# The gated MLP's 42 leftover features as two row tiles, their activations held twice on the partitions

## The chip, the cores and the metric

The kernel runs on one core of a Trainium2 chip. The metric is the device time of one execution in microseconds, as the median of several runs. A core has a matrix engine (TensorE, PE), three engines for elementwise work (VectorE or DVE, ScalarE or ACT, GpSimd or POOL) and a queue for transfers (SyncE or SP). TensorE reads its operands from SBUF, a memory of 128 partitions, and writes to PSUM, which has eight banks of 512 f32 numbers on every partition.

## The reference

The program is an adaptive-norm block on x of shape (2, 2048, 256) in f32: a three-layer transformer with linear attention, then a two-layer transformer with local attention and a gated MLP. The change touches the gated MLP of the second part. Cut to it:

```python
HID = int(256 * 4 * 2 / 3)                  # 682
for l in range(2):
    x = x + local_attention(...) @ wo
    h = layernorm(shift_token(x))
    h = h @ w1 + b1                         # 256 -> 2 * 682
    a, g = jnp.split(h, 2, axis=-1)
    h = a * gelu(g)
    x = x + h @ w2 + b2                     # 682 -> 256
```

682 hidden features are five chunks of 128 and one of 42: `HID_CH = [128] * 5 + [42]`. The 42 are the leftover features of the title.

## The kernel before

The first part (linear attention) takes the first half of the time and is not touched. The second part keeps activations with features on the partitions: a stream tile `s` holds 512 tokens of one batch element, in two halves of 128 features each (`KT = 2`). There are 2 batch elements with 4 blocks of 512 tokens (`B`, `NB`, `TB`), so 8 blocks in each of the two layers.

The MLP (`mlp`, from L1107) walks over tiles (b, n, f): block by block, and in a block over the six chunks f. For each chunk TensorE computes the gate `pg` and the value `pa` from the stream (L1130, two contraction steps each). For the last chunk gate and value stand in one product `pg` of 106 rows: the value on partitions 0 to 41, the gate on 64 to 105 (`G_AT = 64`). ScalarE applies Gelu to the gate (L1138) into a tile `ge`, and VectorE multiplies it with the value plus its bias (L1139), also into `ge`.

The second product (`second`, L1164) multiplies chunk f of `w2` with `ge` and adds it up over the six chunks in two PSUM tiles `acc`, one for each half m of the 256 output features. It is issued one tile late: TensorE's order is the first products of tile i, then the second products of tile i - 1. So between the making of the last `ge` of a block and its use stands the first product of the next block's first chunk. After f = 5, `finish_block` adds `acc`, the bias and the residual on VectorE (L1081, once for each half). In layer 0 the sum is the next layer's stream. In layer 1 it is scaled on ScalarE (L1088), and one tile later `write_block` turns it with eight transposes (`ztp`, L1098), adds the residual (L1102) and writes the result out.

`w2` is a tile of 128 partitions, six chunks and 256 columns. `load_w2` fills it with one transfer for the five full chunks (L198) and one for the 42 leftover rows on partitions 0 to 41 (L201), both on the SP queue: for layer 0 at the start of the second part, for layer 1 from `load_mlp_late` during that layer's attention.

The order on TensorE, VectorE, ScalarE and GpSimd in the second part is the order in which the program issues the instructions (`tc.manual_schedule`). Steps of attention and of the MLP are sorted by due times: `WHEN` for attention, `into`, `FEED` and `out_of` for the MLP. The MLP of layer 0 overlaps the end of its attention and the beginning of layer 1's attention, whose steps used in the prediction are the products `pqkv` (L785), their rotated and normed form `qk` (L854), its transposes `tp` (L864), the scores `sim` (L881) and the running maxima (L897). `sim` takes heads of 64 features in pairs, one on partitions 0 to 63 and one on 64 to 127.

Of the kernel before, what the change touches and what calls it, by code (L numbers as in the profile page):

```python
# [14 lines left out]
P = 128  # L15
KT = 2
# [23 lines left out]
def block_kernel(ctx: ExitStack, tc: tile.TileContext, t: dict, out: bass.AP):  # L40
    nc = tc.nc
# [108 lines left out]
    NFH = len(HID_CH)  # L150

    def load_attn(l):

        wqkv = shared.tile([P, ROOM], F32, tag="wa0", name="wqkv").rearrange("p (k n) -> p k n", k=KT)
        nc.sync.dma_start(wqkv, t["wqkv"][l].rearrange("(k p) n -> p k n", p=P))
        room = shared.tile([P, ROOM], F32, tag="wb0", name="rsn_wo")
        rsn = room[:, : nt * P].rearrange("p (t i d) -> p t i d", i=2, d=64)
        nc.sync.dma_start(rsn, t["rope_s"])
        room2 = shared.tile([P, ROOM], F32, tag="wa1", name="rc_qks")
        rc = room2[:, : nt * P].rearrange("p (t i d) -> p t i d", i=2, d=64)  # L160
        nc.sync.dma_start(rc, t["rope_c"])
        qks = room2[:, nt * P : nt * P + P].rearrange("p (i d) -> p i d", i=2)
        nc.gpsimd.dma_start(qks[:, 0, :], t["q_scale"][l].partition_broadcast(P))
        nc.gpsimd.dma_start(qks[:, 1, :], t["k_scale"][l].partition_broadcast(P))
        wo = room[:, nt * P : nt * P + (INNER // P) * D].rearrange("p (k n) -> p k n", n=D)
        nc.sync.dma_start(wo, t["wo"][l].rearrange("(k p) n -> p k n", p=P))
        return wqkv, rc, rsn, qks, wo

    def scale_tables(rc, rsn, qks):
        for hf in range(2):  # L170
            nc.gpsimd.tensor_tensor(
                rsn[:, :, :, 32 * hf : 32 * hf + 32],
                rsn[:, :, :, 32 * hf : 32 * hf + 32],
                qks[:, :, 32 * (1 - hf) : 32 * (1 - hf) + 32].unsqueeze(1).to_broadcast([P, nt, 2, 32]),
                ALU.mult,
            )
        nc.vector.tensor_tensor(rc, rc, qks.unsqueeze(1).to_broadcast([P, nt, 2, 64]), ALU.mult)


    AW, GW = HID_CH[0] * (NFH - 1), HID_CH[-1]  # L180
    G_AT = 64
# [14 lines left out]
    def load_w2(pool, l):  # L196
        w2 = pool.tile([P, NFH, D], F32, tag="w2", name="w2")
        nc.sync.dma_start(  # L198
            w2[:, : NFH - 1, :], t["w2"][l, :AW, :].rearrange("(k p) n -> p k n", p=P)
        )  # L200
        nc.sync.dma_start(w2[:GW, NFH - 1, :], t["w2"][l, AW:, :])  # L201
        return w2

    attn_w, mlp_w = {}, {}
# [2 lines left out]
    with ExitStack() as c1:  # L207
# [16 lines left out]
        with tc.tile_pool(name="pro", bufs=1) as pro:  # L224
# [8 lines left out]
            for l in range(LA):  # L233
# [3 lines left out]
                for room, at, name, kts, width in (  # L237
# [7 lines left out]
                    w = room[:, at : at + kts * width].rearrange("p (k n) -> p k n", k=kts)  # L245
# [446 lines left out]
    with ExitStack() as c2:  # L692
# [7 lines left out]
        def bank(name):  # L700
            return psum.tile([P, TB], F32, tag="ps", name=name, bufs=8)
# [21 lines left out]
        for i in range(2):  # L723
            nc.gpsimd.tensor_copy(win_r[:, i * P : (i + 1) * P], win[:, (1 - i) * P : (2 - i) * P])
        w2s = {0: load_w2(wp, 0)}
        streams = [entry, {}]
        mids = [{}, {}]
# [4 lines left out]
        def v(l, name, i=0, rows_=P):  # L732
            o = V_F + l * VF_N + VF[name] + i
            return vec[:rows_, o : o + 1]

        def load_mlp_late(l):
            mlp_w[l] = load_mlp(l)
            w2s[l] = load_w2(wp, l)
# [330 lines left out]
        def finish_block(l, b, n, acc):  # L1069
            y = mids[l][b, n]  # L1070
            last = l == LF - 1
            if not last:
                nxt = streams[l + 1]
                z = new_stream(b, n, nxt.get((b, n - 1)))
                zr = rows(z)
                nxt[b, n] = z
            else:
                z = work.tile([P, KT, TB], F32, tag="w4", name="z")
                zr = [z[:, 0, :], z[:, 1, :]]
            for m in range(KT):  # L1080
                nc.vector.scalar_tensor_tensor(  # L1081
                    zr[m], acc[m], v(l, "b2", m), rows(y)[m], ALU.add, ALU.add
                )
            if last:
                xt = work.tile([P, NCH, D], F32, tag="w4", name="xl")
                nc.sync.dma_start(xt, xmid[b, n])
                for m in range(KT):
                    nc.scalar.activation(zr[m], zr[m], AF.Identity, scale=mod[:, 5, m, b : b + 1])  # L1088
                return zr, xt

        def write_block(b, n, zr, xt):
            res = work.tile([P, NCH, D], F32, tag="w4", name="res")
            for c2_ in range(NCH // 2):
                tp = bank("ztp").rearrange("p (u d) -> p u d", u=2)
                for u in range(2):
                    c = 2 * c2_ + u
                    for m in range(KT):
                        nc.tensor.transpose(  # L1098
                            tp[:, u, m * P : (m + 1) * P], zr[m][:, c * P : (c + 1) * P], ident
                        )  # L1100
                half = slice(2 * c2_, 2 * c2_ + 2)
                nc.vector.tensor_tensor(res[:, half, :], tp, xt[:, half, :], ALU.add)  # L1102
            nc.sync.dma_start(
                out[b, n * TB : (n + 1) * TB, :].rearrange("(c p) d -> p c d", p=P), res
            )

        def mlp(l):  # L1107


            tiles = [(b, n, f) for b in range(B) for n in range(NB) for f in range(NFH)]  # L1110
            ge, ready = {}, None
            w1, w2 = mlp_w[l], w2s[l]
            for i, (b, n, f) in enumerate(tiles):
                if l + 1 < LF and i == NFH:
                    attn_w[l + 1] = load_attn(l + 1)
                if l + 1 < LF and i == 3 * NFH:
                    scale_tables(*attn_w[l + 1][1:4])
                hb, w = streams[l][b, n], HID_CH[f]
                pg = bank("pg")
                if f < NFH - 1:  # L1120
                    pa = bank("pa")
                    parts = ((pg, AW + f * P, P), (pa, f * P, P))
                    gate = pg
                else:
                    pa = pg
                    parts = ((pg, 2 * AW, G_AT + GW),)
                    gate = pg[G_AT : G_AT + w, :]
                for pt, off, m in parts:
                    for kt in range(KT):
                        nc.tensor.matmul(  # L1130
                            pt[:m, :],
                            w1[:, kt, off : off + m],
                            hb[:, kt * TB : (kt + 1) * TB],
                            start=(kt == 0),
                            stop=(kt == KT - 1),
                        )
                ge[i] = ap_.tile([P, TB], F32, tag="ge", name="ge", bufs=3)
                nc.scalar.activation(ge[i][:w, :], gate, AF.Gelu, bias=v(l, "b1g", f, w))  # L1138
                nc.vector.scalar_tensor_tensor(  # L1139
                    ge[i][:w, :], pa[:w, :], v(l, "b1a", f, w), ge[i][:w, :], ALU.add, ALU.mult  # L1140
                )
                if ready:
                    write_block(*ready)
                    ready = None
                if i > 0:
                    ready = second(l, i - 1, tiles[i - 1], ge.pop(i - 1), w2)
                yield
            if l + 1 < LF:
                nc.scalar.preload_act_table_set("natural_log_exp_and_others")
            ready = second(l, len(tiles) - 1, tiles[-1], ge.pop(len(tiles) - 1), w2)  # L1150
            if ready:
                yield
                write_block(*ready)
# [3 lines left out]
        def second(l, i, tile_, g, w2):  # L1157
            b, n, f = tile_
            w = HID_CH[f]
            if f == 0:  # L1160
                accs[0] = [bank("acc") for _ in range(KT)]
            acc = accs[0]
            for m in range(KT):
                nc.tensor.matmul(  # L1164
                    acc[m],
                    w2[:w, f, m * P : (m + 1) * P],
                    g[:w, :],
                    start=(f == 0),
                    stop=(f == NFH - 1),
                )  # L1170
            if f == NFH - 1:
                done = finish_block(l, b, n, acc)
                return done and (b, n, *done)
# [144 lines left out]
```

## Time and profile before

| What | Value |
|---|---|
| Median of three runs | 3013.61 us (3012.41 to 3014.05) |
| Time of the profiled execution | 3012.11 us |
| Its span from the first to the last instruction | 3010.3 us |
| TensorE busy | 2927.8 us, 97% |
| VectorE, ScalarE, GpSimd busy | 1679.1, 1345.9, 1065.0 us |
| Second products of the 128-feature chunks (L1164) | 320 records, 150.4 us busy |
| Second products of the 42-feature chunk (L1164) | 64 records, 31.7 us busy |
| Gate and value of the 42-feature chunk (L1130) | 64 records, 30.2 us busy |

A line of a group names source line, engine, operation, output and input tiles, the shape, the number of records, the busy time, and the mean length of one. An f32 product shows as two records. TensorE's records overlap, [...] so the busy time of a group says more than the mean length of a record. PEld is the loading of the stationary operand. In the chain of waits each line is a stretch of the path that ended last.

### The profile page before, as it was taken

Reading aid. Unit: us, or ns where it says so; the run is one execution under the profiler, and the core shown is the slowest. Engines: PE = TensorE matmul, PEld = TensorE weight load, DVE = VectorE, ACT = ScalarE, POOL = GpSimd, SP = SyncE. Lnnn points to the kernel's source line nnn. Section 1 sums busy time; section 2 is a strip of 40 time slices with the busy share of each in tenths; the row PEclk is TensorE's granted clock in tenths of the full one; section 3 lists DMA queues with packets and bytes.
Section 4 is the critical chain, followed back from the end, with each engine's and each line's share of the span. In section 5 each row is a group of like instructions: output and inputs, shape, how many; then the busy total and the mean of one; then the engine's idle time right before and its main releaser. Section 6 shows DMA issues by size and latency. Waiting matters only on the chain.

```text
span 3010.3 us, 49194 instructions
## 1 busy us (share of the span) xinstructions
PE 2927.8 (97%) x19356; PEld 2138.0 (71%) x19356; DVE 1679.1 (56%) x4178; ACT 1345.9 (45%) x3269; POOL 1065.0 (35%) x937
## 2 busy tenths in 40 slices
PE   6999999999999999999996999999999999999999
PEld 5788888888888888788883777775444777776444
DVE  5555565555565555655544777774224777774222
ACT  3333343334443343433333667665114667665211
POOL 2222233222332223322224666663002666663000
PEclk9999999999999999999997999999999999999999
DMA  5000010000100001001012000001000000000011
GB/s 183 1 1 1 1 39 19 1 1 1 36 22 1 1 1 36 22 1 43 16 41 76 1 2 1 1 2 57 0 0 10 20 1 2 1 1 8 28 42 35
DMA packets 37288, 57.10 MB, mean 19 GB/s; under 512 B 3693, under 2 KB 28609, under 8 KB 36545
## 3 DMA queue, kind: packets, MB, share of 16 engines
q1 hardware_dynamic: 36176, 52.37, 5.3%
q8 instruction: 153, 2.51, 0.3%
q0 software_dynamic: 464, 0.54, 0.1%
q10 hardware_dynamic: 416, 1.05, 0.1%
q14 instruction: 79, 0.64, 0.1%
HBM read 41.37 MB, written 12.58 MB: 18 GB/s over the span
## 4 chain that ended last, share of the span: by engine, by line
PE 89%; DVE 4%; ACT 3%; POOL 2%; DMA 1%; issue 1%; SPq 1%; ACTq 0%; DVEq 0%; POOLq 0%
PE acc L630 10%; PE pf L619 10%; PE pqkv L785 10%; PE pg L1130 5%; PE acc L1164 5%; PE pq L409 5%; PE pa L1130 4%; PE av L974 4%; PE sim L881 3%; PE ptp L948 3%; PE po L993 3%; PE sc L495 3%; PE nd L567 3%; PE pu L448 3%; PE pv L425 3%; PE po L597 3%
## 5 line engine op out<-in xcount | busy, mean ns | idle before, releaser
L630 PE MATMUL acc<-wb,fr 128*128 128x256 f32 x1536 | 397.3, 381 | 5.5 <-ACT fr L627 5.1
L619 PE MATMUL pf<-h,wa 128*128 128x256 f32 x1536 | 400.2, 384 | 1.1 <-ACT h L370 0.7
L627 ACT ACTIVATE fr<-pf,vec 128x256 f32<-128x256 f32 x384 | 180.5, 471 | 425.6 <-PE pf L619 424.9
L785 PE MATMUL pqkv<-wqkv,s 128*128 128x512 f32 x768 | 357.9, 602 | 8.2 <-issue 8.2
L501 DVE TENSOR_TENSOR att<-sc,cst 128x512 f32<-128x512 f32 x384 | 238.4, 683 | 157.5 <-PE sc L495 157.5
L630 PEld LDWEIGHTS acc<-wb,fr 128*128 128x128 f32 x1536 | 287.8, 190 | 52.1 <-ACT fr L627 8.6
L379 POOL TENSOR_TENSOR res<-dn,brow 128x512 f32<-128x512 f32 x112 | 144.8, 1292 | 485.4 <-DVE dn L356 483.8
L619 PEld LDWEIGHTS pf<-h,wa 128*128 128x128 f32 x1536 | 275.8, 190 | 55.8 <-issue 19.5
L936 POOL TENSOR_TENSOR pm<-pm,sum 128x1024 f32<-128x1024 f32 (+1 forms) x128 | 235.8, 1842 | 178.2 <-DVE sum L931 178.2
L921 ACT ACTIVATE pm<-pm,mx 128x256 f32<-128x256 f32 (+1 forms) x512 | 249.5, 489 | 58.2 <-DVE mx L913 57.0
L785 PEld LDWEIGHTS pqkv<-wqkv,s 128*128 128x128 f32 x768 | 138.0, 193 | 135.8 <-issue 133.9
L1139 DVE SCALAR_TENSOR_TENSOR ge<-pa,vec,ge 128x512 f32<-128x512 f32 x80 | 60.1, 751 | 298.1 <-PE pa L1130 249.7
L827 POOL TENSOR_TENSOR rot<-raw,rsn_wo 128x512 f32<-128x512 f32 x128 | 160.5, 1275 | 185.4 <-ACT raw L808 185.4
L1138 ACT ACTIVATE ge<-pg,vec 128x512 f32<-128x512 f32 x96 | 65.9, 687 | 325.1 <-PE pg L1130 325.1
L421 ACT ACTIVATE xs<-xs 64x512 f32<-64x512 f32 x192 | 120.7, 629 | 152.1 <-DVE xs L420 142.7
L1130 PE MATMUL pg<-s,w 128*128 128x512 f32 (+1 forms) x384 | 182.2, 597 | 0.0
L1164 PE MATMUL acc<-ge,w 128*128 128x512 f32 (+1 forms) x384 | 182.0, 596 | 0.0
L409 PE MATMUL pq<-h,wa 128*128 128x256 f32 x768 | 175.3, 381 | 0.0
L420 DVE TENSOR_TENSOR xs<-pq,vec 64x512 f32<-64x512 f32 x192 | 132.2, 689 | 76.4 <-PE pq L409 72.6
L409 PEld LDWEIGHTS pq<-h,wa 128*128 128x128 f32 x768 | 146.1, 191 | 21.1 <-issue 1.4
L849 POOL TENSOR_TENSOR qk<-qk,rot 128x1024 f32<-128x1024 f32 x64 | 151.5, 2368 | 0.5
L1130 PE MATMUL pa<-s,w 128*128 128x512 f32 x320 | 150.4, 592 | 0.0
(162 smaller groups left out, 5362.6 us busy)
## 6 DMA issues: line engine op xcount, KB each, us to landing
xin<-in_x_dram SPq DMA_DIRECT2D x32, 256.0 KB, 2.8
x<-res SPq DMA_DIRECT2D x16, 256.0 KB, 2.1
h<-hm SPq DMA_DIRECT2D x16, 256.0 KB, 2.4
s<-h SPq DMA_DIRECT2D x16, 256.0 KB, 5.6
xl<-x SPq DMA_DIRECT2D x8, 512.0 KB, 4.4
out_dram<-res SPq DMA_DIRECT2D x8, 512.0 KB, 3.2
w<-in_w_dram SPq DMA_DIRECT2D x6, 640.0 KB, 4.0
wa<-in_W_dram SPq DMA_DIRECT2D x3, 1024.0 KB, 9.7
```

Source lines behind the costliest of these rows:

```text
L409: nc.tensor.matmul(pq[:, g, :], W[wn, l][:, kt, g * P : (g + 1) * P], h[:, kt, :], start=(kt == 0), stop=(kt == KT - 1),)
L501: nc.vector.tensor_tensor(am, scs[i].rearrange("p g q c -> p (g q) c"), caus.unsqueeze(1).to_broadcast([P, 2 * KT, P]), ALU.mult,)
L619: nc.tensor.matmul(pf, W["W1", l][:, kt, f * P : (f + 1) * P], h1[:, kt, :], start=(kt == 0), stop=(kt == KT - 1),)
L627: nc.scalar.activation(fr[f], pf, AF.Relu, bias=v("bf1", f))
L630: nc.tensor.matmul(acc[:, c, :], fr[f - 1][:, c * P : (c + 1) * P], W["W2", l][:, f - 1, :], start=(f == 1 and c == 0), stop=(f == NF), sk ...
L785: nc.tensor.matmul(pq, s[:, kt * TB + c * P : kt * TB + (c + 1) * P], wqkv[:, kt, i * INNER : (i + 1) * INNER], start=(kt == 0), stop=(kt ...
L827: nc.gpsimd.tensor_tensor(rot[:, :, :, lo : lo + 32], got["raw"][:, :, :, hi : hi + 32], rsn[:, ti, :, lo : lo + 32].unsqueeze(2).to_broad ...
L849: nc.gpsimd.tensor_tensor(got["qk"], got["qk"], got["rot"], ALU.add)
L921: nc.scalar.activation(pm[:, hd, :], pm[:, hd, :], AF.Exp, bias=of("mx", hg)[:, hd : hd + 1], accum_out=of("sum", hg)[:, hd : hd + 1],)
L936: nc.gpsimd.tensor_tensor(pm, pm, of("sum", hg).unsqueeze(2).to_broadcast([P, 4, kw]), ALU.mult)
L1130: nc.tensor.matmul(pt[:m, :], w1[:, kt, off : off + m], hb[:, kt * TB : (kt + 1) * TB], start=(kt == 0), stop=(kt == KT - 1),)
L1164: nc.tensor.matmul(acc[m], w2[:w, f, m * P : (m + 1) * P], g[:w, :], start=(f == 0), stop=(f == NFH - 1),)
```

## The change

The leftover chunk of `w2` is laid out differently: the rows for output half 0 stay on partitions 0 to 41, the rows for half 1 go to partitions 64 to 105. After the product of gate and value of the leftover chunk, VectorE copies the 42 rows of `ge` to partitions 64 to 105 of the same tile. The second product of that chunk reads weights and activations from partitions 0 to 41 for half 0 and from 64 to 105 for half 1. What is added up is the same.

```diff
@@ load_w2
-        nc.sync.dma_start(w2[:GW, NFH - 1, :], t["w2"][l, AW:, :])
+
+        for m in range(KT):
+            nc.sync.dma_start(
+                w2[G_AT * m : G_AT * m + GW, NFH - 1, m * P : (m + 1) * P],
+                t["w2"][l, AW:, m * P : (m + 1) * P],
+            )
         return w2
@@ mlp
                 nc.vector.scalar_tensor_tensor(
                     ge[i][:w, :], pa[:w, :], v(l, "b1a", f, w), ge[i][:w, :], ALU.add, ALU.mult
                 )
+                if f == NFH - 1:
+                    nc.vector.tensor_copy(ge[i][G_AT : G_AT + w, :], ge[i][:w, :])
                 if ready:
                     write_block(*ready)
                     ready = None
@@ second
             for m in range(KT):
+
+                rs_ = slice(G_AT * m, G_AT * m + w) if f == NFH - 1 else slice(0, w)
                 nc.tensor.matmul(
                     acc[m],
-                    w2[:w, f, m * P : (m + 1) * P],
-                    g[:w, :],
+                    w2[rs_, f, m * P : (m + 1) * P],
+                    g[rs_, :],
                     start=(f == 0),
                     stop=(f == NFH - 1),
                 )
```

## The prediction

> **What bounds the kernel now.** The page's first row gives TensorE 97% of the span, so I went to the stage that the change touches. The table by stretches for two windows of the MLP stage of layer 0 (us, then the busy time and number of instructions of TensorE, weight loads, VectorE, ScalarE, GpSimd):
>
> ```profile
> 2130.00:2160.00 30.00, 30.00 (x70) 12.86 (x69) 8.62 (x10) 4.12 (x6) 0.18 (x1) 1.00 0.00 1
> 2310.00:2340.00 30.00, 28.57 (x155) 16.75 (x155) 20.82 (x63) 21.26 (x56) 17.96 (x15) 1.00 0.09 24
> ```
>
> In the first window TensorE never rests and VectorE works 8.6 of 30 us; every other window between 2100 and 2310 and between 2770 and 2980 also shows TensorE at 30.00. There a TensorE microsecond saved is a microsecond gained. In the second, where layer 0's MLP hands over to layer 1's attention, TensorE waits 1.4 us, and a saving may vanish.
>
> Next the groups by shape, to see what a record is and what row tiles cost:
>
> ```profile
> L619 PE MATMUL pf<-h,wa 128*128 128x256 f32 x1536 | 400.2, 384 | 1.1 <-ACT h L370 0.7 <-DVE att L501 0.3
> L881 PE MATMUL sim<-kT,qT 64*128 64x256 f32 x960 | 120.4, 389 | 0.0
> L1164 PE MATMUL acc<-ge,w 42*128 42x512 f32 x64 | 31.7, 615 | 0.0
> ```
>
> The touched products are the last row: 2 layers x 8 blocks x 2 output halves are 32 matmuls, shown as 64 records, so each f32 matmul is two records. A full-array record of 256 columns occupies 400.2/1536 = 0.261 us; one of line 881, which alternates two row tiles of 64 partitions, 120.4/960 = 0.125. The same columns cost 0.48 times as much where two row tiles lie side by side.
>
> The chain of waits (start and length of each piece, us), at the touched products of a middle block, at line 881, and at layer 0's last block:
>
> ```profile
> 2275.91 1.72 PE pa L1130 x4
> 2277.63 1.91 PE acc L1164 x4
> 2279.54 1.91 PE pg L1130 x4
> ...
> 2305.49 0.87 PE tp L864 x8
> ...
> 2308.08 1.09 PE sim L881 x16
> 2309.17 1.90 PE pg L1130 x4
> ...
> 2314.72 1.93 PE acc L1164 x4
> 2316.71 0.63 issue
> 2317.34 1.21 DVE qk L854
> ```
>
> Four full records of 512 columns take 1.72 us, 0.43 each. The touched four take 1.91 and the group after them 1.91 again: entering and leaving costs 0.19 each, and the four still run one after another. Line 881 pays the same toll (1.90 for the group after it), but its 16 records of 128 columns take 1.09, or 0.90 without the toll, against 0.87 for only 8 full-array records of that width on line 864. The last three lines show where TensorE is not the bound: the path leaves TensorE at 2316.71 and goes through VectorE.
>
> The timeline around a block in layer 1 (start, length, engine, line):
>
> ```profile
> 2968.95 0.74 DVE L1139 SCALAR_TENSOR_TENSOR ge<-pg,vec,ge 42x512 f32<-42x512 f32 x1 [3.33 <-ACT ge L1138]
> ...
> 2973.28 1.98 PE L1164 MATMUL acc<-ge,w 42*128 42x512 f32 x4
> ...
> 2974.44 1.61 DVE L1081 SCALAR_TENSOR_TENSOR z<-acc,vec,s 128x512 f32<-128x512 f32 x2 [0.23 <-PE acc L1164]
> 2975.19 1.98 PE L1130 MATMUL pg<-s,w 128*128 128x512 f32 x4
> ...
> 2978.72 1.04 PE L1098 MATMUL ztp<-cst,z 128*128 128x128 f32 x8
> ```
>
> The activation is ready at 2969.69 and read at 2973.28. The end of the chain:
>
> ```profile
> 2998.65 3.64 PE acc L1164 x8
> 3002.29 0.03 issue
> 3002.31 0.76 DVE z L1081
> ```
>
> Here nothing lies between the last block's touched products and the epilogue. Last, the entry to this phase on the DMA queue:
>
> ```profile
> 1592.07 0.52 SPq L685 DMA_DIRECT2D h<-hm  x1
> 1592.64 0.64 SPq L201 DMA_DIRECT2D w<-in_w_dram  x1
> 1596.25 9.40 SPq L719 DMA_DIRECT2D s<-h  x16
> ```
>
> The queue then stands for 3 us until the write of h has landed, which the first s load waits for.
>
> **What the Trainium skill says.** "TensorE: Matmul & The Clock Gate", Part 3 (Packing small matmuls), says that matmuls whose operands start in different row groups run at the same time; line 881 agrees (0.125 against 0.261). "TensorEngine Tiling (Array Packing)", Key Properties: changing the tiling mode drains the engine. The 0.19 on both sides of the touched products agrees, and shows that they already run in a row-tiled mode, so the change adds no switch that is not paid today. The same page, Gotcha 1, forbids two row tiles in one PSUM bank at once; the two halves accumulate in two tiles, each a bank of its own (512 f32 columns). "VectorE: DVE Perf Modes", perf-mode tier table, puts an f32 copy from SBUF at twice the rate of one from PSUM; the trace has 420 ns for 128x512 from SBUF (L274) and 692 from PSUM (L956).
>
> **The change, part by part.**
>
> The pair. Today four slots of 0.43 in a row. If the two halves pair like line 881's, two slots remain: 2 x 0.43 = 0.86 saved per block; entry and exit stay. What follows must be ready 0.86 earlier. In layer 1 the transposes ztp follow two groups later and need both z and their scaling on ScalarE: the second z starts at 2975.30 (2974.44 + 1.61 - 0.75), its scaling ends at 2976.80 (L1088), and ztp would come at 2977.86 instead of 2978.72, still 1.06 later. No reader gets late, and banks are freed by VectorE and ScalarE work that is done by then. Seven of eight blocks in each layer lie in stretches with TensorE at 30.00: 14 x 0.86 = 12.0 us gained.
>
> Layer 0's last block. After the pair come pqkv (1.72) and then tp (2318.61), which waits for VectorE's qk (L854), itself queued behind the two z (L1081). The first z waits for the first half, whose end does not move (two slots as before). The second starts at 2316.67 today (2315.81 + 1.61 - 0.75), 0.86 after the first, because its half ends that much later; with both halves done together it starts when the first z is finished, 0.75 after. So tp gains 0.1, and the rest of the 0.86 turns into a longer wait: count 0.1 (0 to 0.86).
>
> The last block of all. Same shape: the second z moves from 0.86 to about 0.75 after the first, gaining 0.1. The second half now waits for the copy as well: it would start some 0.45 after the first half, and still end before the first z does. If the first half is held until the second may start, 0.35 is lost: count 0.1 gained (from 0.35 lost to 0.15 gained).
>
> The copies. Sixteen of 42x512, SBUF to SBUF, on VectorE right after L1139. Nearest row: 420 ns (L274); upper end 692 (L956); I take 0.42. In 15 blocks it ends at about 2970.15 on the block above, 3.1 us before the reader at 2973.28: TensorE's work on the next tile hides it. Queued behind it on VectorE is the next L1139, idle until 2973.45. At layer 0's last block it pushes the maxima of L897 by 0.42 (they end at 2314.46 and VectorE then idles to 2315.81), so the z are not touched. Without that cover each copy would cost 0.4 to 0.7. Count 0.
>
> The loads. Two more DMA issues on the SP queue, one per layer; each 42x256 load becomes two of 42x128, the same bytes. At the phase's entry the extra issue (0.64 as L201 took) fits in the 3 us for which the queue stands; the s loads keep their time. 0, at most 0.3 if the landing of w2 disturbs h. In layer 1 it has 400 us of attention to hide in. The orders of the instructions on TensorE, ScalarE and GpSimd do not change; VectorE gains the 16 copies only.
>
> Sum: 12.0 + 0.1 + 0.1 = 12.2 off the profiled span of 3010.3, to 2998.1. That execution took 3012.11 with what lies around the span, 1.5 under the median of the runs; I take the same 12.2 off the median: 3013.61 - 12.2 = 3001.4.
>
> **The rivals.**
>
> Half a pairing. If a half's two passes go ahead in order and only the inner two overlap (first alone, two together, last alone), three slots remain: 14 x 0.43 + 0.2 = 6.2 off, 3007.4. Against it: line 881 would then need five slots for eight records, 0.62 of the full-array price, and shows 0.48. For it: line 881 has several pairs in a row, here stands one alone, and it accumulates onto earlier products.
>
> No pairing: the halves run one after another; about 3013.6, unchanged. For it only that 42 of 64 rows is a shape that no paired product here has.
>
> Slower: alternating without overlap. If the passes alternate between the row tiles but do not overlap, and each alternation pays the 0.19 toll, a block makes three alternations more: 3 x 0.19 = 0.57 in 14 blocks is 8.0, time 3021.6. It decides once the alternations cost over the 0.86 saved less whatever still overlaps. Against it: line 881 alternates between every two records and pays the toll once in and once out.
>
> **How the numbers follow.** Full pairing 0.86, half 0.05, none 0.04, slower 0.05. Its own range: all sixteen blocks gain 0.86 (13.8 off: 2999.8) to a hand-over or load that gives back 3 us (3004.4), with 1 us either way as the runs before scatter by 1.6: 2998.8 to 3005.4. That alone holds about 0.82, so the range stops there. A measurement tells 0.2% (6.0 us) from no change. Full pairing is faster; half a pairing sits on the border and is split; so faster 0.88, same 0.07, slower 0.05.
>
> **What would show it.** Right: the touched group in the chain falls from 1.91 to about 1.05, with the following group still at 1.91; its busy time falls from 31.7 to about 17; blocks stand 0.86 closer; VectorE has 16 copies near 0.42; the wait of tp on L854 at the hand-over grows to about 1.0. Wrong: records of the two halves 0.43 apart, a touched group of 1.5 or more, tolls between the halves, or TensorE waiting for the copy in a middle block.

## The result, and the profile after

The changed kernel takes 3001.97 us (median of 6 runs, 3000.0 to 3003.34) against 3013.56 us before (median of 6): ratio 0.996, 95% interval 0.995 to 0.997. The profiled span goes from 3010.3 to 2998.2 us. The change added lines, so line numbers shift: L1164 is now L1173, L1139 is L1144, L1081 is L1086, L881 is L886, L854 is L859 and L864 is L869; the copy is L1148.

The groups by shape of the changed kernel (busy us, mean ns, idle time ahead):

```profile
L886 PE MATMUL sim<-kT,qT 64*128 64x256 f32 x960 | 120.4, 389 | 0.0
L1173 PE MATMUL acc<-ge,w 42*128 42x512 f32 x64 | 18.5, 641 | 0.0
L1148 DVE COPY ge<-ge 42x512 f32<-42x512 f32 x16 | 8.3, 518 | 0.5
```

The touched products fell from 31.7 to 18.5 us with the same 64 records; the prediction said about 17, though its own 16 x 0.86 off 31.7 give 17.9. The copies add up to 8.3 us on VectorE, with a mean of 518 ns; that mean hides one outlier, as the next views show. The chain of waits (start, length, what):

```profile
2270.83 1.72 PE pa L1135 x4
2272.55 1.06 PE acc L1173 x4
2273.60 1.91 PE pg L1135 x4
...
2306.10 0.66 DVE ge L1144
2306.78 1.98 DVE ge L1148
...
2310.66 1.31 DVE s L1086 x2
2311.97 1.13 DVE qk L859
```

In the middle of the MLP the group of four touched records takes 1.06 instead of 1.91, and the group after it 1.91 as before: two slots are gone and the toll is the same. By their starts the four records stand at 0, 0.007, 0.533 and 0.540 us and the next group begins at 1.059; before, they stood at 0, 0.533, 0.962 and 1.391, and the next group began at 1.911. The two halves run at the same time. At the hand-over from layer 0 to layer 1 the path now goes through VectorE and through a copy of 1.98 us.

The timeline around the block of layer 1 that was shown of before:

```profile
2959.14 0.42 DVE L1148 COPY ge<-ge 42x512 f32<-42x512 f32 x1
...
2962.69 1.13 PE L1173 MATMUL acc<-ge,w 42*128 42x512 f32 x4
...
2963.75 1.98 PE L1135 MATMUL pg<-s,w 128*128 128x512 f32 x4
2963.85 1.41 DVE L1086 SCALAR_TENSOR_TENSOR z<-acc,vec,s 128x512 f32<-128x512 f32 x2 [0.23 <-PE acc L1173]
...
2967.29 1.04 PE L1103 MATMUL ztp<-cst,z 128*128 128x128 f32 x8
```

The copy ends 3.1 us before its reader, ztp does not wait, and the two z follow each other without a gap (1.41 instead of 1.61 for both). The timeline of the hand-over, first of the kernel before:

```profile
2311.95 0.74 DVE L1139 SCALAR_TENSOR_TENSOR ge<-pg,vec,ge 42x512 f32<-42x512 f32 x1
2312.08 2.35 POOL L849 TENSOR_TENSOR qk<-qk,rot 128x1024 f32<-128x1024 f32 x1
...
2314.65 1.98 PE L1164 MATMUL acc<-ge,w 42*128 42x512 f32 x4
...
2318.61 1.09 PE L864 MATMUL tp<-cst,qk 128*128 128x128 f32 x8
```

Then of the changed kernel:

```profile
2306.14 2.35 POOL L854 TENSOR_TENSOR qk<-qk,rot 128x1024 f32<-128x1024 f32 x1
...
2306.78 1.98 DVE L1148 COPY ge<-ge 42x512 f32<-42x512 f32 x1
...
2308.72 1.23 PE L1173 MATMUL acc<-ge,w 42*128 42x512 f32 x4
...
2313.15 1.09 PE L869 MATMUL tp<-cst,qk 128*128 128x128 f32 x8 [1.29 <-DVE qk L859]
```

The copy starts while GpSimd is at work and ends 0.27 us after GpSimd's instruction (2308.49). What stands behind it on VectorE is late by the rest. TensorE itself is held a little too: the second half of this pair starts 0.10 us after the first instead of 0.007, because the copy ends only at 2308.76. tp comes 4.43 us after the start of the touched products; before it was 3.95. The end of the chain of the changed kernel, then the transposes in the timelines of the kernel before and of the changed one:

```profile
2987.21 2.78 PE acc L1173 x7
...
2990.02 0.76 DVE z L1086
...
2990.80 1.39 ACT z L1093 x2
```

```profile
3003.87 1.50 PE L1098 MATMUL ztp<-cst,z 128*128 128x128 f32 x7 [0.53 <-ACT z L1088]
```

```profile
2992.24 0.98 PE L1103 MATMUL ztp<-cst,z 128*128 128x128 f32 x7 [0.33 <-ACT z L1093]
```

The seven transposes after the first took 1.50 us before and take 0.98 now. TensorE's clock was granted at half from 3004.2 on before, in the middle of them, and from 2994.0 on now, after the last. Last, the DMA queue at the entry to this part of the program:

```profile
1592.57 1.04 SPq L203 DMA_DIRECT2D w<-in_w_dram  x2
...
1596.17 8.79 SPq L724 DMA_DIRECT2D s<-h  x15
```

The issue of the second load of w2 ends at 1593.61, inside the stretch for which the queue stands; the s loads start where they did.

Where the time went, from the starts of the records (us). A block is marked by the start of its touched products, block 0 to 7 in layer 0 and 8 to 15 in layer 1:

| Stretch | Before | After | Difference | Prediction |
|---|---|---|---|---|
| block 0 to block 7 | 214.55 | 208.58 | -5.97 | -6.02 |
| block 7 to tp (hand-over) | 3.95 | 4.43 | +0.48 | -0.1 |
| tp to block 8 (attention of layer 1) | 471.97 | 471.94 | -0.03 | 0 |
| block 8 to block 15 | 209.72 | 203.76 | -5.96 | -6.02 |
| block 15 to the end | 10.03 | 9.36 | -0.67 | -0.1 |
| sum | | | -12.15 | -12.24 |

### The profile page after: what moved, and what is told of

It is laid out like the page before. It is cut to its first block, busy times and chain, and to the rows that moved or that the text cites. A ratio compares the mean times of both kernels' runs of the same rounds, so it can differ in the third digit from the quotient of the medians.

```text
span 2998.2 us, 49213 instructions
## 1 busy us (share of the span) xinstructions
PE 2914.3 (97%) x19356; PEld 2132.3 (71%) x19356; DVE 1686.0 (56%) x4194; ACT 1344.5 (45%) x3269; POOL 1065.1 (36%) x937
## 4 chain that ended last, share of the span: by engine, by line
PE 88%; DVE 4%; ACT 3%; POOL 2%; DMA 1%; issue 1%; SPq 1%; DVEq 0%; ACTq 0%; POOLq 0%
PE acc L635 11%; PE pf L624 10%; PE pqkv L790 10%; PE pg L1135 5%; PE pq L414 5%; PE acc L1173 5%; PE pa L1135 4%; PE av L979 4%; PE sim L886 3%; PE ptp L953 3%; PE po L998 3%; PE sc L500 3%; PE nd L572 3%; PE pu L453 3%; PE pv L430 3%; PE po L602 3%
## 5 line engine op out<-in xcount | busy, mean ns | idle before, releaser
L1144 DVE SCALAR_TENSOR_TENSOR ge<-pa,vec,ge 128x512 f32<-128x512 f32 x80 | 60.1, 751 | 281.9 <-PE pa L1135 230.6
L1173 PE MATMUL acc<-ge,w 128*128 128x512 f32 (+1 forms) x384 | 168.8, 600 | 0.0
L854 POOL TENSOR_TENSOR qk<-qk,rot 128x1024 f32<-128x1024 f32 x64 | 151.5, 2367 | 0.5
```

What stands on the lines that cost most here:

```text
L854: nc.gpsimd.tensor_tensor(got["qk"], got["qk"], got["rot"], ALU.add)
L1173: nc.tensor.matmul(acc[m], w2[rs_, f, m * P : (m + 1) * P], g[rs_, :], start=(f == 0), stop=(f == NFH - 1),)
```

## The experiments

The stretch ahead of the second part moves by up to 5 us from run to run, because TensorE's clock falls to half for one or two more short windows there, as in the run of the experiment with the doubled product (1508.9 to 1515.8). So a few tenths are read from the first of the MLP's second products to the end of the trace: 942.91 us before, 930.77 after, and 930.78 in a second profile of the changed kernel.

**The copies without the pairing.** Both halves read partitions 0 to 41 again; the copies stay.

```diff
-        for m in range(KT):
-            nc.sync.dma_start(w2[G_AT * m : G_AT * m + GW, NFH - 1, m * P : (m + 1) * P], ...)
+        nc.sync.dma_start(w2[:GW, NFH - 1, :], t["w2"][l, AW:, :])
...
-                rs_ = slice(G_AT * m, G_AT * m + w) if f == NFH - 1 else slice(0, w)
+                rs_ = slice(0, w)
```

> The change without its pairing: the 16 copies on VectorE stay, but both output halves read partitions 0 to 41, and w2 is loaded as before. Theory (the gain is the two row tiles lying side by side, the copies are hidden except at layer 0's last block): touched group back to 1.91 us in the chain, busy about 31.7 us; time that of the kernel before plus about 0.5 us for the late copy at the hand-over, so 3013.5 to 3014.5. Rival (the gain is from the loads or from the new order of waits): still near 3002.

Measured: 3015.18 us against 3014.30 for the kernel before on the same chip, ratio 1.0 (0.9991 to 1.0008). The group by shape, and the timeline at the hand-over:

```profile
L1168 PE MATMUL acc<-ge,w 42*128 42x512 f32 x64 | 31.7, 615 | 0.0
```

```profile
2314.97 1.99 DVE L1143 COPY ge<-ge 42x512 f32<-42x512 f32 x1
...
2316.91 1.98 PE L1168 MATMUL acc<-ge,w 42*128 42x512 f32 x4
...
2321.33 1.09 PE L864 MATMUL tp<-cst,qk 128*128 128x128 f32 x8 [0.52 <-DVE qk L854]
```

The busy time is back at 31.7 and the seven blocks at 214.54 us. This kernel also loads w2 as before, so the run alone doesn't tell the pairing from the loads. The table does: the gain lies in the two stretches of MLP blocks, in which no load of w2 is issued. So the gain in the blocks is the pairing. tp comes 4.42 us after block 7's products, as with the change (4.43): the 0.47 us lost at the hand-over belong to the copy. The stretch to the end is 943.59, 0.68 more than before: 0.47 there and 0.25 after the last block, where all the transposes after the first fall into the halved clock (from 3006.4).

**GpSimd kept busy beside five copies.** A product of 128x1024 on GpSimd, started by a small copy on ScalarE after the Gelu, in layer 0's blocks 2 to 6.

```diff
                 nc.scalar.activation(ge[i][:w, :], gate, AF.Gelu, bias=v(l, "b1g", f, w))
+                if f == NFH - 1 and l == 0 and 2 <= i // NFH < 7:
+                    busy = work.tile([P, 2 * TB], F32, tag="w4", name="busy")
+                    nc.scalar.copy(busy_t[:, :1], vec[:, :1])
+                    nc.gpsimd.tensor_tensor(busy, hb[:, : 2 * TB], busy_t[:, :1].to_broadcast([P, 2 * TB]), ALU.mult)
```

> The change, and in layer 0's blocks 2 to 6 a product of 128x1024 on GpSimd (about 2.4 us, its result is not used) that starts with the Gelu of the leftover chunk. Theory (the copy waits while GpSimd works): these five copies take 1.5 to 2.2 us instead of 0.42, ending about 0.3 us after GpSimd's instruction; the others keep 0.42. TensorE does not wait for them, so the span moves by less than 0.3 us. Rival (the long copy belongs to the hand-over itself): all of these copies keep 0.42.

Measured in one run (3002.27 us): the five copies took 1.52 to 1.56 us, the copy at the hand-over 1.99, the ten others 0.42. The timeline of one of the five:

```profile
2184.78 1.89 POOL L1147 TENSOR_TENSOR busy<-s,busy_t 128x1024 f32<-128x1024 f32 x1 [19.87 <-ACT busy_t L1146]
...
2185.43 1.52 DVE L1154 COPY ge<-ge 42x512 f32<-42x512 f32 x1
...
2188.98 1.13 PE L1180 MATMUL acc<-ge,w 42*128 42x512 f32 x4
```

GpSimd ends at 2186.67 and the copy at 2186.95, 0.28 later, as at the hand-over. It did not matter which block it was; it mattered that GpSimd was at work. The blocks stayed 28.72 us apart (208.58 over seven): in the middle of the MLP even a copy of 1.5 us is covered. The span missed its forecast: the stretch to the end is 930.34, 0.43 less than with the change, where less than 0.3 was expected. Nearly all of it comes at one group of transposes (ptp, L953) in layer 1's attention, some 400 us behind the last of the five copies; what moved it is open. "SBUF — State Buffer" of the Trainium skill, section "Who interferes with whom", says just this: a VectorE copy between two SBUF places in its fast mode and a GpSimd instruction want the same port pair, and the later of the two stands still until the other is done. The runs agree, and in both directions: GpSimd's small copy (L713), which comes while VectorE's long copy is still at work at the hand-over, took 0.38 us, against 0.17 before the change (L708) and 0.19 in the run without a copy at the hand-over (L715).

**The product computed twice instead of copied.** A second multiplication from PSUM takes the copy's place (0.74 us, where the copy takes 0.42); only the very last block of the program, marked by end, keeps the copy.

```diff
+                if f == NFH - 1 and not end:
+                    nc.vector.scalar_tensor_tensor(
+                        ge[i][G_AT : G_AT + w, :], pa[:w, :], v(l, "b1a", f, w), ge[i][:w, :], ALU.add, ALU.mult
+                    )
                 nc.vector.scalar_tensor_tensor(ge[i][:w, :], pa[:w, :], v(l, "b1a", f, w), ge[i][:w, :], ALU.add, ALU.mult)
-                if f == NFH - 1:
+                if f == NFH - 1 and end:
                     nc.vector.tensor_copy(ge[i][G_AT : G_AT + w, :], ge[i][:w, :])
```

> In place of each copy VectorE computes the product of gate and value a second time from PSUM into partitions 64 to 105 (first, then the one in place); the very last block keeps its copy. Theory (at layer 0's last block the copy took 1.98 us because it reads SBUF twice as fast through something that GpSimd held at the time): every second product takes 0.74 us, also at the hand-over, the first sum s of L1086 there starts as soon as the first half is done, and tp comes about 3.9 us after the touched products' start instead of 4.43; span 0.5 to 0.6 us shorter than the changed kernel's 2998.2. Rival (VectorE waited there for something else, such as a semaphore): an instruction of about 2 us stays at the hand-over and the span is the same or longer.

Measured: 3002.77 us, ratio 0.996 (0.9946 to 0.9974). The timeline at the hand-over:

```profile
2309.74 2.35 POOL L854 TENSOR_TENSOR qk<-qk,rot 128x1024 f32<-128x1024 f32 x1
...
2309.74 0.74 DVE L1146 SCALAR_TENSOR_TENSOR ge<-pg,vec,ge 42x512 f32<-42x512 f32 x1
...
2310.51 0.74 DVE L1150 SCALAR_TENSOR_TENSOR ge<-pg,vec,ge 42x512 f32<-42x512 f32 x1
...
2311.40 1.95 PE L790 MATMUL pqkv<-wqkv,s 128*128 128x512 f32 x4 [0.96 <-DVE ge L1150]
...
2317.04 1.09 PE L869 MATMUL tp<-cst,qk 128*128 128x128 f32 x8 [0.71 <-DVE qk L859]
```

Both multiplications take 0.74 beside a GpSimd instruction that runs from 2309.74 to 2312.09, so the long copy is gone. tp follows the touched products by 3.75 us: less than 4.43, and less than before the change. But the span did not get shorter: the pqkv ahead of the touched products now waits 0.96 us for the second multiplication. It reads nothing that the multiplications write, so what it waits for must be the PSUM bank that both of them read; the trace does not name banks. Block 0 to block 7 took 209.55 instead of 208.58; this wait also gave VectorE time to catch up, so the 3.75 is not a gain by itself. The stretch to the end is 931.06, 0.3 longer than with the copy. The theory of the wait held; the expected gain was taken by the wait ahead of the products.

**The hand-over's block left unpaired.** Layer 0's last block has no copy and runs on partitions 0 to 41 (an extra load of its w2 rows is not shown).

```diff
-                if f == NFH - 1:
+                if f == NFH - 1 and (l, b, n) != (0, B - 1, NB - 1):
                     nc.vector.tensor_copy(ge[i][G_AT : G_AT + w, :], ge[i][:w, :])
...
-                rs_ = slice(G_AT * m, G_AT * m + w) if f == NFH - 1 else slice(0, w)
+                two = f == NFH - 1 and (l, b, n) != (0, B - 1, NB - 1)
+                rs_ = slice(G_AT * m, G_AT * m + w) if two else slice(0, w)
```

> The change, but layer 0's last block has no copy and runs its two halves one after another on partitions 0 to 41 (its w2 rows are loaded there too). Theory (the pairing gains nothing in that block, and its copy, held for 1.98 us by GpSimd, costs 0.47 us): tp comes 3.95 us after the start of the touched products, as before the change, instead of 4.43; everything else as in the changed kernel, so 0.5 us less. Rival (the copy's delay is hidden as the prediction had it, and the 0.86 of the pairing counts there too): 4.7 us or more, and the kernel gets slower by 0.4 us or more.

Measured: 3000.77 us beside 3002.38 of the changed kernel on the same chip; the runs of the two overlap, so the trace decides. tp follows by 3.95 us and the stretch to the end is 930.23, 0.54 less than with the change:

```profile
2311.00 1.98 PE L1176 MATMUL acc<-ge,w 42*128 42x512 f32 x4
...
2314.95 1.09 PE L871 MATMUL tp<-cst,qk 128*128 128x128 f32 x8
```

With the copies but no pairing it was 4.42, with both 4.43. So at the hand-over the copy costs half a microsecond, and the pairing beside it gains nothing. The changed kernel, run again beside this one:

> The changed kernel again, beside the next two on one chip: ratio 0.996 to the kernel before, all theories.

Measured: ratio 0.9958 (0.9945 to 0.9972).

**No row tiles at all.** The leftover chunk runs over the full array, with the other 86 rows zero.

```diff
+        nc.gpsimd.memset(w2[:, NFH - 1, :], 0.0)
+        nc.sync.dma_start(w2[:GW, NFH - 1, :], t["w2"][l, AW:, :])
...
+                if f == NFH - 1:
+                    nc.gpsimd.memset(ge[i], 0.0)
                 nc.scalar.activation(ge[i][:w, :], gate, AF.Gelu, bias=v(l, "b1g", f, w))
...
-                rs_ = slice(G_AT * m, G_AT * m + w) if f == NFH - 1 else slice(0, w)
+                rs_ = slice(0, P)
```

> No pairing and no copy: the leftover chunk's second products run over all 128 partitions, with zeros in the other 86 rows of w2 and ge (GpSimd clears ge ahead of the Gelu). Theory (0.19 us is lost entering a row-tiled stretch and 0.19 leaving it): the touched group and the one after it take 1.72 us each in the chain, 0.38 to 0.40 less per block; 14 to 16 blocks make 5.5 to 6.3 us, time about 3007.5 to 3008.5. Rival (the 0.19 is due to the 42 rows, the accumulation's end or the bank change, not to the array's mode): 1.91 stays, time 3013.5.

Measured: 3009.76 us against 3014.30 before on the same chip, ratio 0.9984 (0.9976 to 0.9991). The chain at the leftover chunk's products of block 3 and the group after them:

```profile
2189.09 1.72 PE acc L1169 x4
2190.81 1.72 PE pg L1131 x4
```

Both groups take 1.72, so the toll does not come from the end of the accumulation or from the change of banks, which are the same here. It goes with products of few rows: line 881 with 64 rows pays it, line 1164 with 42 too, and the 128 rows here do not. The array's mode and the number of rows change together in this run, so it can't tell these two apart. From block 8 to block 14 it saves 0.39 for each of six blocks (182.70 to 180.36). In layer 0 it saves only 1.48 of some 2.7 in seven blocks, for at the hand-over the clearing of ge stands behind GpSimd's attention work and pqkv waits 1.23 us for what follows from it. The total, 4.70 on the stretch to the end, is therefore under the 5.5 expected. The same run helps with the end of the program. Its last block is not paired, and its last seven transposes are these:

```profile
3000.90 0.98 PE L1099 MATMUL ztp<-cst,z 128*128 128x128 f32 x7 [0.53 <-ACT z L1089]
```

They wait 0.53 us for the scaling, as before the change, but take 0.98 instead of 1.50: here the clock fell only at 3004.0, after them.

**Two pairs next to each other.** In every second block the leftover chunk comes first, and the pair of the block ahead is held back to stand beside it.

```diff
-            tiles = [(b, n, f) for b in range(B) for n in range(NB) for f in range(NFH)]
+            tiles = [(b, n, f) for b in range(B) for n in range(NB)
+                     for f in ((NFH - 1, *range(NFH - 1)) if n % 2 else range(NFH))]
...
-                if i > 0:
-                    ready = second(l, i - 1, tiles[i - 1], ge.pop(i - 1), w2)
+                for k in (i - 2, i - 1):
+                    if k not in ge or (k == i - 1 and tiles[k][2] == NFH - 1 and not tiles[k][1] % 2):
+                        continue
+                    ready = second(l, k, tiles[k], ge.pop(k), w2) or ready
...
+            head, tail = (NFH - 1, NFH - 2) if n % 2 else (0, NFH - 1)
...
-                    start=(f == 0),
-                    stop=(f == NFH - 1),
+                    start=(f == head),
+                    stop=(f == tail),
```

> The change, with the leftover chunk taken first instead of last in every second block, so that the pairs of two neighbouring blocks stand next to each other on TensorE (the first block's pair is held back by one tile). Theory (the toll is paid per stretch of row-tiled products, not per pair): the eight records of two pairs take 0.19 + 4 x 0.43 = 1.9 us and the group after them 1.91, so 0.39 less per two blocks, 8 times 3.1 us; and no leftover chunk stands at the hand-over any more, which gives the 0.86 of that block and takes the held copy away. Together 4 to 4.5 us under the changed kernel. Rival (each pair pays the toll, or the third live ge tile and the four accumulators make TensorE wait): no gain, or slower than the changed kernel.

Measured: 2997.39 us (2995.47 to 2997.79), ratio 0.9941 (0.9928 to 0.9955). The chain, then the two groups:

```profile
2962.80 1.92 PE acc L1181 x8
2964.72 1.91 PE pg L1140 x4
```

```profile
L1181 PE MATMUL acc<-ge,w 42*128 42x512 f32 x64 | 15.9, 615 | 0.0
```

```profile
L1153 DVE COPY ge<-ge 42x512 f32<-42x512 f32 x16 | 6.7, 421 | 0.5
```

Eight records take 1.92 where two separate pairs took 2 x 1.06, and the group after them pays its 1.91 once for two blocks. So the toll is paid per stretch of row-tiled products. All sixteen copies take 0.42, as none stands beside GpSimd any more. The stretch to the end is 926.09, 4.7 less than with the change and 16.8 less than before. Up to tp at the hand-over the gain over the change is 2.94 (four tolls of 0.39 and the 0.86 and 0.47 of the hand-over would be 2.9), behind it 1.74 (four tolls would be 1.56). This is the fastest kernel of the study.

## Why the prediction was right, and where it was not

The forecast of 3001.4 us and a span of 2998.1 met 3001.97 and 2998.2. The mechanism of the main term was right; that the sum fits to 0.1 us is luck, as the steps show:

- **The pair.** 14 x 0.86 = 12.0 was forecast, 5.97 + 5.96 = 11.9 measured. The inference from line 881 (two row tiles in 0.48 of the time) and from the toll that was already paid carried over to 512 columns and to accumulating products. The run without pairing and the table by stretches show that this is the whole gain in the blocks. The rivals of half a pairing, no pairing and alternation fall with the starts of the records: 0.007 us apart, no toll between them.
- **The hand-over.** Forecast: 0.1 gained; measured: 0.48 lost. The step that failed is "I take 0.42" for the copy there, with 0.69 as the upper end: it took 1.98. The copy was priced by its own row and its cover (VectorE idle from 2314.46 to 2315.81), without asking what GpSimd does at that moment. The timeline of before had it: GpSimd's L849 runs from 2312.08 to 2314.43, and a copy behind L1139 would start at about 2312.7. The maxima behind the copy ended at 2310.57, after the first half of the products was done, and pushed both sums and qk. The rest of the step held: the 0.86 of that block did turn into a longer wait of tp for L859 (1.29, forecast about 1.0). The profile of before had also shown such a wait on another instruction, in the timeline at the start of layer 0's attention:

```profile
1622.64 2.36 POOL L849 TENSOR_TENSOR qk<-qk,rot 128x1024 f32<-128x1024 f32 x1
...
1624.20 0.82 DVE L913 TENSOR_SCALAR mx<-mx 128x4 f32<-128x4 f32 x1
```

  Of the 128 records of line 913, 125 take 0.15 to 0.17. The three others (0.82, 1.12, 1.12) are the only ones that started when L849 had more than 0.2 us to run, and each ended within 0.03 us of its end.
- **The last block.** Forecast: 0.1 gained; measured: 0.67. About 0.2 is the pairing: the second half started 0.36 after the first, with the copy (forecast 0.45), and the transposes that wait for the second z came 3.38 us after the block's start instead of 3.58. The forecast had half of that, because it let the second z start 0.75 after the first; it started 0.67 after. Another 0.36 lies between that transpose and the last one (1.08 us before, 0.71 after), in which the clock was halved before and not after. The full-array run shows that this part is the clock's: unpaired, with that transpose at 3.58 too, it takes 0.71 there at the full clock. The rest, 0.1, lies behind the last transpose and is not explained. In all nine traces every stretch at one granted clock, except the last one, which ends with the trace, lasts a whole number of steps of 3.41 us (the last one at full speed 402 before, 399 after). Where the transposes stand against these steps is chance.
- **Copies in the other blocks, loads.** Forecast 0; the tables and the queue show 0 or close to it (-0.03). The copy's price away from GpSimd, 0.42, was the right one; it was the trace's own (420 ns from SBUF beside 692 from PSUM is a factor of 1.65, not the two quoted in the prediction). The run with GpSimd busy shows that even 1.5 us is covered in the middle of the MLP.

So the total was met because the prediction's main term was right, while two small terms of opposite sign, +0.58 at the hand-over and -0.57 at the end, cancelled by luck. The first was a mistake that the profile of before could have prevented. Of the second, 0.36 is the clock, which was not foreseeable and is no gain of the change.

## What to carry to other kernels

If a chunk of few rows (42 here) has two outputs, and the trace shows the toll of a row-tiled mode around it, the second row tile costs TensorE nothing: half of the slots go, here 0.86 us a pair, for one copy of the activations. Put such pairs next to each other, because the toll of 0.4 us was paid per stretch here and not per pair. Before pricing a VectorE copy or scaling between SBUF places, look at what GpSimd does in the same microsecond, and give the work to a block where nothing waits behind it.

## What was not expected of the hardware

- A 42x512 copy on VectorE took 0.42 us alone. When a GpSimd product of 128x1024 was running at its start, it took 1.52 to 1.99 us and ended about 0.3 us after that product. The multiplication of the same size with an operand in PSUM kept its 0.74 us beside GpSimd.
- The same 42-row products, unpaired, cost less over the full array with zeros (1.72 and 1.72) than row-tiled (1.91 and 1.91): the toll came to 0.39 us a block.
- A pair whose second half waits does not hold the first: at the end of the program the second half started 0.36 us late, and the second record of the first half still started at 0.533 us, as in the other pairs.
